# A decoder of four layers on one core: the order of the first loads, the clearing of the routing buffers, and the bias rows

## The chip, the cores and the metric

The kernel runs on one core of a Trainium2 chip. The metric is the device time of one execution in microseconds. A core has five engines that run side by side, each with its own stream of instructions in a fixed order: TensorE (PE, matrix products, with PEld for its weight loads), VectorE (DVE), ScalarE (ACT), GpSimd (POOL) and SyncE (SP), which here issues most of the transfers. An instruction that has to wait for a semaphore holds up everything behind it on its engine.

## The reference

The reference is a decoder on x of shape 8 x 256 x 256 (eight elements, 256 tokens, width 256) with a context of 8 x 256 x 192. It has four blocks, each of a self attention, a cross attention and a feed forward part; after each of these twelve parts the result is added to x and normalised:

```python
x = _layernorm(x + _L0_attn_ref(x, ...), axis=-1)
x = _layernorm(x + _L0_xattn_ref(x, ctx_768, ...), axis=-1)
x = _layernorm(x + _L0_ffn_ref(x, ...), axis=-1)
...
x = _layernorm(x + _L3_ffn_ref(x, ...), axis=-1)
return x
```

The kernel calls each of the twelve parts a layer and numbers them from 0 in the code. In the text of this document they are counted from one: layer one is `l0_attn` (16 heads of width 16, with biases on the queries, keys and values), layer two `l0_xattn` (one head, keys and values from the context), layer three `l0_ffn` (eight experts of width 512, all computed for all tokens and weighted by a softmax), layer four `l1_attn`, layer eight `l2_xattn`, layer ten `l3_attn` (its scores get a bias by relative position, looked up in a table of 32 buckets for 16 heads), layer eleven `l3_xattn` and layer twelve `l3_ffn` (two of eight experts for each token; the tokens are sorted by expert into a buffer in device memory, `slots`, and the results go to another, `given`).

## The kernel before

All eight elements of x stay on the core as tiles `xs[b]` (128 partitions, two halves of 128 tokens, 256 wide) through all layers. Besides them each layer keeps `xT`, the transposed x, in four tiles of two elements each. `transpose_x(b, name)` makes one element's share: four PE transposes of 128 x 128 into a bank of the accumulators (PSUM) and one copy out of it. Inside stretches whose DVE order is written out by hand (`order_of_text`) that copy is made by ACT; elsewhere `evac` alternates between DVE and ACT.

Weights come through a ring of six tiles of 1 MB each (`wtile`, `wload`, `wpart`, line 117 for all their transfers), so that SP runs ahead until a tile of the ring is still in use. Rows that are added along the tokens come through four smaller tiles (`load_row`, line 101), columns of biases through `load_cols` (line 95). All of these transfers, and those of x, the context and the clears, are issued by SP in one order; the program builder works it out before the run from the text and from when each transfer's target comes free, and it stands fixed in the program. The orders of PE, DVE, ACT and POOL are fixed in the same way, with those inside `order_of_text` taken from the text.

The start, before layer one: `hc`, a small table, and the eight x tiles are loaded (lines 90 and 108); then all eight elements are transposed (tiles `xtr_in`, `xT_in`), then the context, transposed (`ctxT`, lines 1754 and 1756, 2 MB; used by layers eight and eleven only). Layer one's weights follow (`w0a`, in the order wq, wk, wv, wo), then its bias columns and rows.

Layer one, `attention16` (called for layers one, four and seven), works on blocks of half an element: 16 blocks, each of four steps. `project_qk` and `proj_tok` make the queries, keys and values of the next element (tiles pk, pq, pv), `step` computes the scores twice, once with the queries along the partitions (s) for the row maxima (nm, by DVE) and once with the keys (t), on which ACT takes the exponential (eT); `turn_maxima` transposes the maxima on PE (ntr), `less_max` folds them into the queries (qm), `attend` multiplies the exponentials with the values and with ones (av), `normalise` divides. The previous element's output projection (po), addition of x (`add_x`; xb = x + bo by POOL), norm statistics (st, mv by DVE; ve and rs by POOL) and transposes (`finish`) are spread between the steps. The transposes of x, ntr and the projections take turns on one pair of PSUM banks in this layer.

The biases of the queries and keys are prepared by POOL (`kb`, lines 884 and 887). POOL also prepares columns for later layers when the builder places them early: `bqs` of layer two (line 914) and `bm` of layer four (line 870) stand, in POOL's order, ahead of the third element's xb and the first element's ve and rs.

Layer two begins, before its loop over elements, with `clear_slots` (lines 896 to 901): POOL sets a tile of the ring to zero, and SP writes it to the 16 MB of `slots` in 16 transfers of 1 MB and to the last 1 MB of `given` in a seventeenth. The products of layer twelve need this at the far end of the kernel.

Layer three goes over the eight experts, each with two tiles of the ring (w2a with Wg and Wu, w2b with Wd), and within an expert over four pairs of elements: pg and pu on PE, the product of the two on DVE, py on PE.

`relative_bias` runs at the start of layer eight: two small loads (`w9r`: a table of one-hot buckets and the embedding), one matmul (pb, line 1371), one copy, a transfer that writes the 16 resulting rows 128 times each to device memory (`lines`, 4 MB, line 1375), and four transfers that read windows of it, shifted by one from partition to partition, into the bias tile of layer ten (line 1379).

Of the kernel before, what the change touches and what calls it, by code (L numbers as in the profile page):

```python
# [11 lines left out]
F32 = mybir.dt.float32  # L12
# [7 lines left out]
P = 128  # L20
B, S, D, C = 8, 256, 256, 192
NT = S // P
# [10 lines left out]
def decoder_kernel(ctx: ExitStack, tc: tile.TileContext, t: dict, out: bass.AP, run=range(12)):  # L33
# [70 lines left out]

    xs = []
    for b in range(B):
        xb = xpool.tile([P, NT, D], F32, tag=f"x{b}", name=f"x{b}")
        nc.sync.dma_start(out=xb, in_=t["x"][b].rearrange("(t p) d -> p t d", p=P))
        xs.append(xb)
    xT = [None] * NB2  # L110
    xT_next = [None] * NB2

# [230 lines left out]
    ALL_KEYS = [(0, 0, S), (1, S, 2 * S)]  # L343


    def attention16(li, kind, wq, wk_, wv, wo, tabs=None, kbias=None, bv=None, bo=None, last=False):

# [9 lines left out]
        with tc.tile_pool(name=f"wk{li}", bufs=2) as wk:  # L357
# [164 lines left out]
            with order_of_text(mybir.EngineType.PE, mybir.EngineType.DVE):  # L522
                for k in (1, 0):
                    leave_qk(0, k, project_qk(0, k))
                for s in range(4):
                    step(-1, s)
                project_v(0)
                tr = turn_maxima(0)
                for e in range(2):
                    less_max(0, e, tr)  # L530
                for i, (b, c) in enumerate(blocks):
                    more = b + 1 < B
                    if c == 0:
                        step(i, 0, lambda: normalise(i - 1, 0))
                        normalise(i - 1, 1)
                        if more:
                            pk = project_qk(b + 1, 1)
                        step(i, 1)
                        if more:
                            leave_qk(b + 1, 1, pk)  # L540
                            pq = project_qk(b + 1, 0)
                    else:
                        step(i, 0)
                        if b > 0:
                            norm_scaled(ys.pop(b - 1))
                        attend(i - 1, 1, (1,))
                        step(i, 1, lambda: normalise(i - 1, 0))
                        normalise(i - 1, 1)
                        if more:
                            pv = proj_tok(wv, xTb(b + 1), 0, f"pv_{li}_{b + 1}")  # L550
                    step(i, 2)
                    if more:
                        if c == 0:
                            leave_qk(b + 1, 0, pq)
                        else:
                            leave_v(b + 1, pv)
                    if c == 1:
                        attend(i, 0, (0, 1))
                    elif b > 0:
                        po = project_out_mm([aTs.pop(b - 1)], wo, f"{li}_{b - 1}")  # L560
                        ys[b - 1] = add_x(wk, b - 1, po, bo, f"{li}_{b - 1}")
                    step(i, 3)
                    if c == 0:
                        attend(i, 0, (0, 1))
                    elif b > 0:
                        finish(b - 1, f"l{li}", last)
                    if i + 1 < len(blocks):
                        tr = turn_maxima(i + 1)
                        less_max(i + 1, 0, tr)
# [304 lines left out]
        return tabs  # L874

    def l0_attn(last):
        wq, wk_, wv, wo = weights16("w0a", [t[f"L0_attn_{n}"] for n in ("wq", "wk", "wv", "wo")])

        kbias = const.tile([P, 4, 2], F32, tag="kb0", name="kb0")
        for i, n in enumerate(("bq", "bk")):  # L880
            col = load_cols(f"L0_attn_{n}", 2)
            for e in range(2):
# [3 lines left out]
                if n == "bk":  # L886
                    nc.gpsimd.tensor_tensor(kbias[:, 2 + e, :], kbias[:, 2 + e, :],
                                            hc[:, 2 + e:3 + e].to_broadcast([P, 2]), ALU.add)
        attention16(0, "bias", wq, wk_, wv, wo, kbias=kbias.rearrange("p i c -> p (i c)"),
                    bv=load_row("L0_attn_bv", D), bo=load_row("L0_attn_bo", D), last=last)  # L890

    def clear_slots():

        routed["clear"] = True
        zero = wtile("zero")
        nc.gpsimd.memset(zero, 0.0)
        n = E8 * B * S // 16
        for i in range(16):
            nc.sync.dma_start(out=slots[i * n:(i + 1) * n].rearrange("(p r) d -> p (r d)", p=P), in_=zero)

        nc.sync.dma_start(out=given[ALWAYS * 256:].rearrange("(p r) d -> p (r d)", p=P), in_=zero)

    def l0_xattn(last):
        w = wtile("w0x")
# [8 lines left out]
        bqs = const.tile([P, 2], F32, tag="bqs1", name="bqs1")  # L913
        nc.gpsimd.tensor_scalar(bqs, bq, 1.0 / 16.0, None, ALU.mult)
        bv = load_row("L0_xattn_bv", D)
        clear_slots()
        with tc.tile_pool(name="wk1", bufs=3) as wk:
            for b in range(B):
                nm = f"1_{b}"
# [31 lines left out]
    def l0_ffn(last):  # L951
        NF = 4
        wr = load_router("L0_ffn_gate_w")
        with tc.tile_pool(name="wk2", bufs=2) as wk:
            gates = []
            for p in range(NB2):
# [401 lines left out]
            norm_and_transpose(b, xs[b], "l8", last)  # L1358
            xT[b // 2] = xT_next[b // 2]

    def relative_bias():

        W = S + P
        w = wtile("w9r")
        hot, emb, line = w[:32, 0:512], w[:32, 512:528], w[:16, 1024:1536]
        wload(hot, t["buckets"])
# [1 line left out]
        pb = bank("mm", "pb9")  # L1370
        nc.tensor.matmul(pb[:16, :], emb, hot, start=True, stop=True)
# [35 lines left out]
    def route_setup():  # L1407
# [20 lines left out]
        nc.gpsimd.iota(place_no, pattern=[[P, NT]], base=0, channel_multiplier=1,  # L1428
                       allow_small_or_imprecise_dtypes=True)
        if "clear" not in routed:  # L1430
            clear_slots()
# [308 lines left out]
    def ctx_weights(w, c0, n, wk_, wv):  # L1740
# [7 lines left out]
            got.append(w[tl][:, c:c + n])  # L1748
        return got

    with banks():
        for b in range(B):
            transpose_x(b, "in")
    nc.sync.dma_start(out=ctxT[:, 0, :], in_=t["ctxT"][0:P])
# [6 lines left out]
    pool9, rel9 = [], []  # L1761
    for i in run:
# [141 lines left out]
```

## Time and profile before

| what | value |
|---|---|
| median of three runs | 3599.01 us (3598.97 to 3599.45) |
| the profiled execution's own time | 3600.19 us |
| its span, first to last instruction | 3598.5 us |
| granted TensorE clock, mean | 0.972 |
| PE busy | 3361.3 us (93%) |
| DVE, ACT, POOL busy | 1643.1, 1054.2, 839.5 us |
| moved by the transfers | 168.37 MB |
| layer one's matmuls | from 21.50 us to 257 us |
| first matmul of layer three | 344.43 us |
| pb in layer eight | 2004.60 us |

The page of a profile gives busy times by engine and, in 40 slices of 90 us, how busy each engine and the transfers were. Of the other views, the timeline lists instructions in the order of time, with what ended the idle time before each; the waits add these idle times up; the windows give the busy times in chosen stretches. "SPq" is the issuing of a transfer by SP, which is not counted as busy; a transfer goes on long after its issue. An engine that waits costs nothing by itself. What costs is a wait that PE, which is the busiest engine throughout, takes over.

### The profile page before, as it was taken

To read this page: it belongs to the slowest core of one execution; us is meant where nothing else is said; L and a number is where in the kernel's file an instruction comes from. 1 tells how busy PE (TensorE), PEld (TensorE's weight loads), DVE (VectorE), ACT (ScalarE), POOL (GpSimd) and SP (SyncE) were. 2 spreads that over 40 slices of the span, in tenths; PEclk is the share of its full clock that TensorE was granted. 3 is DMA by queue.
4 is the path that set the end of the run, shared out by engine and by line. 5 is a ranking of instruction groups with operands and counts; after the bars stand their busy time and mean duration, and the time that the engine had idled before them with its cause. 6 is when DMAs were issued, how large, how long until landed. Compare 5 with 4: busy or idle time off the path is not lost. (4 is left out here: it accounts for less than half of the span.)

```text
span 3598.5 us, 49729 instructions
## 1 busy us (share of the span) xinstructions
PE 3361.3 (93%) x20476; PEld 2403.8 (67%) x20476; DVE 1643.1 (46%) x3154; ACT 1054.2 (29%) x2567; POOL 839.5 (23%) x883
## 2 busy tenths in 40 slices
PE   7989999999999978899998899899998999989998
PEld 4556655655556546688766676677776777768887
DVE  4764222222258756521388455766664454531003
ACT  3432111111113335532233342234343443321111
POOL 1000000000010046622122332222223343432214
PEclk8999899999999989999999999999999999999999
DMA  8000000000000001034300500100001000025542
GB/s 306 2 16 24 7 29 18 18 18 24 16 1 1 2 14 57 1 140 161 108 2 2 97 1 24 36 1 1 1 1 42 1 13 12 13 79 181 189 141 74
DMA packets 63386, 168.37 MB, mean 47 GB/s; under 512 B 7888, under 2 KB 38352, under 8 KB 51440
## 3 DMA queue, kind: packets, MB, share of 16 engines
q1 hardware_dynamic: 47408, 76.15, 7.1%
q0 software_dynamic: 15744, 88.94, 7.0%
q8 instruction: 166, 2.72, 0.3%
q14 instruction: 68, 0.56, 0.1%
HBM read 131.78 MB, written 33.29 MB: 46 GB/s over the span
## 5 line engine op out<-in xcount | busy, mean ns | idle before, releaser
L155 DVE TENSOR_REDUCE nm<-s 128x4 f32<-128x1024 f32 (+2 forms) x448 | 455.7, 1030 | 124.4 <-PE s L160 66.2
L610 POOL TENSOR_TENSOR ex<-ex,urc 128x1024 f32<-128x1024 f32 x192 | 363.3, 1893 | 622.9 <-DVE urc L155 610.9
L601 ACT ACTIVATE ex<-s,nm 128x256 f32<-128x256 f32 (+1 forms) x704 | 337.6, 492 | 341.7 <-DVE nm L155 319.0
L465 ACT ACTIVATE eT<-t 128x1024 f32<-128x1024 f32 (+1 forms) x192 | 182.6, 953 | 366.3 <-PE t L160 366.2
L851 PE MATMUL pu<-xT_l,w2a 128*128 128x512 f32 x512 | 244.4, 600 | 0.0
L851 PE MATMUL pg<-xT_l,w2a 128*128 128x512 f32 x512 | 242.0, 594 | 1.3 <-ACT sg L982 1.3
L160 PE MATMUL s<-qk,qk 32*128 32x256 f32 (+1 forms) x1536 | 218.9, 404 | 26.0 <-DVE nm L155 19.7
L983 DVE TENSOR_TENSOR h<-pu,sg 128x512 f32<-128x512 f32 x128 | 88.6, 692 | 337.2 <-PE pu L851 337.2
L982 ACT ACTIVATE sg<-pg 128x512 f32<-128x512 f32 x128 | 76.4, 597 | 565.7 <-PE pg L851 565.7
L836 PE MATMUL py<-w2b,h 128*128 128x256 f32 x1024 | 226.4, 379 | 0.0
L836 PEld LDWEIGHTS py<-w2b,h 128*128 128x128 f32 x1024 | 194.5, 190 | 40.4 <-issue 15.3
L163 PE MATMUL etr<-ident,ex 128*128 128x128 f32 x1568 | 211.0, 277 | 7.9 <-POOL ex L610 3.4
L160 PE MATMUL t<-qm,qk 32*128 32x256 f32 (+1 forms) x1536 | 207.7, 392 | 7.0 <-DVE nm L155 6.2
L163 PEld LDWEIGHTS etr<-ident,ex 128*128 128x128 f32 x1568 | 177.1, 141 | 51.6 <-issue 33.0
L160 PE MATMUL av<-eT,vg 128*64 128x256 f32 x1536 | 205.7, 393 | 1.7 <-ACT eT L175 1.1
L160 PE MATMUL s<-kg,qg 64*128 64x256 f32 x1280 | 177.9, 396 | 22.9 <-ACT qg L669 11.6
L160 PEld LDWEIGHTS s<-qk,qk 32*128 32x128 f32 x1536 | 126.6, 192 | 95.6 <-issue 49.3
L851 PEld LDWEIGHTS pu<-xT_l,w2a 128*128 128x128 f32 x512 | 98.1, 192 | 122.1 <-issue 122.1
L851 PEld LDWEIGHTS pg<-xT_l,w2a 128*128 128x128 f32 x512 | 97.0, 191 | 108.4 <-issue 105.2
L155 DVE COPY eT<-etr 128x1024 f32<-128x1024 f32 (+1 forms) x116 | 138.8, 1197 | 64.4 <-PE etr L163 64.4
L160 PEld LDWEIGHTS s<-kg,qg 64*128 64x128 f32 x1280 | 116.0, 187 | 74.6 <-ACT qg L669 26.9
L155 POOL TENSOR_SCALAR ve_l<-mv_l 128x2 f32<-128x2 f32 x104 | 23.6, 227 | 568.3 <-DVE mv_l L155 567.6
(336 smaller groups left out, 5949.1 us busy)
## 6 DMA issues: line engine op xcount, KB each, us to landing
slots<-zero SPq DMA_DIRECT2D x16, 1024.0 KB
given<-yo SPq DMA_DIRECT2D x19, 256.0 KB
w2a<-in_L_ffn_Wg SPq DMA_DIRECT2D x8, 512.0 KB
w2a<-in_L_ffn_Wu SPq DMA_DIRECT2D x8, 512.0 KB
w2b<-in_L_ffn_Wd SPq DMA_DIRECT2D x8, 512.0 KB
lines<-w9r SPq DMA_DIRECT2D x1, 4096.0 KB
bias<-lines SPq DMA_DIRECT2D x4, 768.0 KB
x<-in_x SPq DMA_DIRECT2D x8, 256.0 KB
```

The costliest lines, as they stand in the source:

```text
L155: return lambda *args, **kw: in_order(getattr(getattr(nc, self.engine), op)(*args, **kw))
L160: in_order(nc.tensor.matmul(*args, **kw))
L163: in_order(nc.tensor.transpose(*args))
L465: nc.scalar.activation(eT[:, :, :n], tt[:, :, :n], AF.Exp)
L601: nc.scalar.activation(ex[:, g, :], flat[:, g, :], AF.Exp, bias=nm[:, g:g + 1], accum_out=sums[:, g:g + 1])
L610: nc.gpsimd.tensor_tensor(ex, ex, rc[:, :nseg].unsqueeze(2).to_broadcast([P, nseg, 1024 // nseg]), ALU.mult)
L836: nc.tensor.matmul(py[:, q * D:(q + 1) * D], h[:, f, i * P:(i + 1) * P], w2[:, f, :], start=(f == 0), stop=(f == nf - 1))
L851: nc.tensor.matmul(ph, w1[:, c, f * P:(f + 1) * P], xT[p][:, c, :], start=(c == 0), stop=(c == 1))
L982: nc.scalar.activation(sg, pg, AF.Silu)
L983: nc.vector.tensor_tensor(h[:, f, :], pu, sg, ALU.mult)
```

## The change

Five things are moved; nothing is computed differently.

- The first loads. Only x0 is loaded at first and transposed before layer one. Layer one then loads wk and wq, the columns bq and bk, wv with its row bv, x1, wo with its row bo, and then x2 to x7.
- The transposes. x1 is transposed before the blocks of layer one start. x2 to x7 are transposed inside it by the new parameter `arrive` of `attention16`: in the second block of element b, ahead of step 1, for element b + 2. Their copies fall to ACT there.
- `ctxT` is loaded by `load_ctx` ahead of layer three.
- The clears. `clear_slots` gets a tile of layer three's own pool in place of a tile of the ring and returns its 17 transfers as a list; layer three issues one of them ahead of each pair of elements, from expert 0 on, until the list is empty.
- The bias rows. `relative_bias` is cut in two. Its first part, `relative_lines` (loads, matmul, copy, the writing of lines), is called by layer two in the place where the clears were; layer eight keeps the four windowed loads.

```diff
     for b in range(B):
-        xb = xpool.tile([P, NT, D], F32, tag=f"x{b}", name=f"x{b}")
-        nc.sync.dma_start(out=xb, in_=t["x"][b].rearrange("(t p) d -> p t d", p=P))
-        xs.append(xb)
+        xs.append(xpool.tile([P, NT, D], F32, tag=f"x{b}", name=f"x{b}"))
+
+    def bring(b):
+        nc.sync.dma_start(out=xs[b], in_=t["x"][b].rearrange("(t p) d -> p t d", p=P))
+
+    bring(0)
...
                         attend(i - 1, 1, (1,))
+                        if arrive is not None and b + 2 < B:
+                            arrive(b + 2)
                         step(i, 1, lambda: normalise(i - 1, 0))
...
     def l0_attn(last):
-        wq, wk_, wv, wo = weights16("w0a", [t[f"L0_attn_{n}"] for n in ("wq", "wk", "wv", "wo")])
+        w = wtile("w0a")
+
+        def part(i, n):
+            return wpart(w, 512 * i, 2, 256, t[f"L0_attn_{n}"])
+
+
+        wk_, wq = part(0, "wk"), part(1, "wq")
...
+        wv, bv = part(2, "wv"), load_row("L0_attn_bv", D)
+        bring(1)
+        wo, bo = part(3, "wo"), load_row("L0_attn_bo", D)
+        for b in range(2, B):
+            bring(b)
+
+        def arrive(b):
+            transpose_x(b, "in")
+            xT[b // 2] = xT_next[b // 2]
+
+        arrive(1)
...
-    def clear_slots():
+                    bv=bv, bo=bo, last=last, arrive=arrive)
+
+    def clear_slots(zero):
+

         routed["clear"] = True
-        zero = wtile("zero")
         nc.gpsimd.memset(zero, 0.0)
         n = E8 * B * S // 16
-        for i in range(16):
-            nc.sync.dma_start(out=slots[i * n:(i + 1) * n].rearrange("(p r) d -> p (r d)", p=P), in_=zero)
-
-        nc.sync.dma_start(out=given[ALWAYS * 256:].rearrange("(p r) d -> p (r d)", p=P), in_=zero)
+        parts = [slots[i * n:(i + 1) * n] for i in range(16)] + [given[ALWAYS * 256:]]
+        return [lambda to=to: nc.sync.dma_start(out=to.rearrange("(p r) d -> p (r d)", p=P), in_=zero)
+                for to in parts]
...
         bv = load_row("L0_xattn_bv", D)
-        clear_slots()
+        relative_lines()
...
+            clear = clear_slots(wk.tile([P, 2048], F32, tag="zero", name="zero", bufs=1))
             for e in range(E8):
...
                 for p in range(NB2):
+                    if e < 6:
+                        work_off(clear, 1)
...
-    def relative_bias():
-
-
-
-        W = S + P
+    def relative_lines():
+
         w = wtile("w9r")
...
-        bias = pool9[0].tile([P, 16, W], F32, tag="bias", name="bias9")
         lines = dram.tile([16, P, 512], F32, tag="lines", name="lines9")
         nc.sync.dma_start(out=lines, in_=line.unsqueeze(1).to_broadcast([16, P, 512]))
+        rel9.append(lines)
+
+    def relative_bias():
+
+
+        W = S + P
+        if not rel9:
+            relative_lines()
+        lines = rel9.pop()
+        bias = pool9[0].tile([P, 16, W], F32, tag="bias", name="bias9")
...
     with banks():
-        for b in range(B):
-            transpose_x(b, "in")
-    nc.sync.dma_start(out=ctxT[:, 0, :], in_=t["ctxT"][0:P])
-    for i in range(2):
-        nc.sync.dma_start(out=ctxT[64 * i:64 * i + 64, 1, :], in_=t["ctxT"][P:C])
+        transpose_x(0, "in")
...
+        if i > 1 and early:
+
+            load_ctx()
+            early = False
```

More of the change, by code (lines that the diff above doesn't have):

```diff
@@ L343, in decoder_kernel, with attention16 @@
     ALL_KEYS = [(0, 0, S), (1, S, 2 * S)]
-    def attention16(li, kind, wq, wk_, wv, wo, tabs=None, kbias=None, bv=None, bo=None, last=False):
+    def attention16(li, kind, wq, wk_, wv, wo, tabs=None, kbias=None, bv=None, bo=None, last=False,
+                    arrive=None):
         H, d = 16, 16
@@ L888, in l0_attn @@
                                             hc[:, 2 + e:3 + e].to_broadcast([P, 2]), ALU.add)
+        wv, bv = part(2, "wv"), load_row("L0_attn_bv", D)
[7 more added lines that the diff above has]
+        arrive(1)
         attention16(0, "bias", wq, wk_, wv, wo, kbias=kbias.rearrange("p i c -> p (i c)"),
-                    bv=load_row("L0_attn_bv", D), bo=load_row("L0_attn_bo", D), last=last)
-    def clear_slots():
+                    bv=bv, bo=bo, last=last, arrive=arrive)
+    def clear_slots(zero):
         routed["clear"] = True
-        zero = wtile("zero")
         nc.gpsimd.memset(zero, 0.0)
         n = E8 * B * S // 16
-        for i in range(16):
-            nc.sync.dma_start(out=slots[i * n:(i + 1) * n].rearrange("(p r) d -> p (r d)", p=P), in_=zero)
-        nc.sync.dma_start(out=given[ALWAYS * 256:].rearrange("(p r) d -> p (r d)", p=P), in_=zero)
+        parts = [slots[i * n:(i + 1) * n] for i in range(16)] + [given[ALWAYS * 256:]]
+        return [lambda to=to: nc.sync.dma_start(out=to.rearrange("(p r) d -> p (r d)", p=P), in_=zero)
+                for to in parts]
     def l0_xattn(last):
@@ L1430, in route_setup @@
         if "clear" not in routed:
-            clear_slots()
+            work_off(clear_slots(wtile("zero")))
         routed["keep"] = keep
@@ L1749, in ctx_weights, with load_ctx @@
         return got
+    def load_ctx():
+        nc.sync.dma_start(out=ctxT[:, 0, :], in_=t["ctxT"][0:P])
+        for i in range(2):
+            nc.sync.dma_start(out=ctxT[64 * i:64 * i + 64, 1, :], in_=t["ctxT"][P:C])
     with banks():
-        for b in range(B):
-            transpose_x(b, "in")
-    nc.sync.dma_start(out=ctxT[:, 0, :], in_=t["ctxT"][0:P])
-    for i in range(2):
-        nc.sync.dma_start(out=ctxT[64 * i:64 * i + 64, 1, :], in_=t["ctxT"][P:C])
+        transpose_x(0, "in")
+        if run[0] != 0:
+            for b in range(1, B):
+                bring(b)
+                transpose_x(b, "in")
     layers = [l0_attn, l0_xattn, l0_ffn, l1_attn, l1_xattn, l1_ffn,
@@ L1761, in decoder_kernel @@
     pool9, rel9 = [], []
+    early = True
     for i in run:
         xT[:] = xT_next
+        if i > 1 and early:
+            load_ctx()
+            early = False
         if i == 10:
```

## The prediction

> **What bounds the kernel now.** I read the page first, then the timeline of the first 40 us, the table of busy times over chosen windows, PE's waits, and the timelines around the places that the change touches.
>
> ```profile
> span 3598.5 us, 49729 instructions
> ...
> PE 3361.3 (93%) x20476; PEld 2403.8 (67%) x20476; DVE 1643.1 (46%) x3154; ACT 1054.2 (29%) x2567; POOL 839.5 (23%) x883
> ...
> DMA  8000000000000001034300500100001000025542
> ```
>
> PE is busy for 93% of the span, so a gain can only be idle time of PE that goes away. The DMA row shows where to look: the transfers fill one slice, the first 90 us.
>
> The timeline of the start (start us, length us, engine, line, operation; in brackets the idle time before it and what ended it):
>
> ```profile
> 1.25 4.00 SPq L108 DMA_DIRECT2D x<-in_x  x8
> ...
> 5.30 0.84 SPq L1754 DMA_DIRECT2D ctxT<-in_ctxT  x1
> ...
> 8.60 0.37 SPq L117 DMA_DIRECT2D w0a<-in_L_attn_wk  x1
> ...
> 10.76 0.34 SPq L95 DMA_DIRECT2D c_L_attn_bq<-in_L_attn_bq  x1
> ...
> 21.50 3.78 PE L160 MATMUL pk<-xT_in,w0a 128*128 128x256 f32 x8 [7.92 <-DMA w0a<-in_L_attn_wk]
> ...
> 25.38 1.93 ACT L383 ACTIVATE qk<-pk,kb,hc 128x256 f32<-128x256 f32 x4 [12.78 <-POOL xb L332]
> ```
>
> The reader is to see that the first projection, pk, waits for wk until 21.50. Eight x tiles and all of ctxT (2.1 MB each) and wq stand before wk in the one queue.
>
> Then the windows between successive transposes of the maxima (ntr, one per half element). Columns: window, length, busy time and count of PE, PEld, DVE, ACT, POOL, then clock, DMA share, GB/s:
>
> ```profile
> 51.55:63.78 12.23, 10.60 (x143) 6.30 (x139) 8.88 (x14) 4.09 (x4) 0.00 (x0) 1.00 1.01 424
> 63.78:77.95 14.17, 14.17 (x154) 9.27 (x155) 8.78 (x11) 7.73 (x12) 0.00 (x0) 1.00 0.98 398
> 77.95:95.30 17.35, 12.81 (x146) 7.36 (x143) 10.53 (x20) 4.29 (x5) 3.12 (x8) 0.90 0.18 45
> ...
> 121.70:135.88 14.18, 14.18 (x155) 9.28 (x155) 8.78 (x11) 8.01 (x13) 1.27 (x1) 1.00 0.00 1
> 135.88:148.11 12.23, 11.19 (x147) 6.71 (x143) 10.44 (x20) 4.29 (x5) 0.93 (x2) 1.00 0.01 1
> ```
>
> Halves of 14.17 and 12.23 us alternate; the one at 77.95 takes 17.35, that is 17.35 - 12.23 = 5.12 us too much. Its timeline says why:
>
> ```profile
> 80.96 0.34 POOL L870 TENSOR_TENSOR bm_L_attn_bq<-c_L_attn_bq,hc 128x2 f32<-128x2 f32 x2 [46.99 <-DMA c_L_attn_bq<-in_L_attn_bq]
> ...
> 84.48 0.72 POOL L155 TENSOR_TENSOR rs_l<-ve_l,nhalf 128x2 f32<-128x2 f32 x1
> 85.23 0.73 DVE L155 TENSOR_SCALAR x<-y,mv_l,rs_l 128x256 f32<-128x256 f32 x2 [3.51 <-POOL rs_l L155]
> ...
> 88.35 0.80 PE L160 MATMUL s<-qk,qk 32*128 32x256 f32 x2 [3.50 <-DVE nm L155]
> ```
>
> POOL had reached an early operation of layer four (bm), whose bias column stands on SP's queue behind the 17 clears of 1 MB. It sat there for 46.99 us; the first norm's rs was queued behind it, DVE waited 3.51 us, and PE 3.50.
>
> **The change part by part.**
>
> *First transfers.* In the built program's SP order, x1 is the ninth transfer: hc, x0, wk, wq, bq, bk, wv, bv, x1. On PE the transposes of x0 and x1 both stand before pk, so pk waits for x1, not x0 alone. Bytes up to x1: five of 0.262 MB and bv's 0.131, 1.44 MB. In the trace, windows of 1 us moved 0.45 MB by 4.0, 0.71 by 5, 1.02 by 6, 1.37 by 7, 1.70 by 8: 1.44 MB at 7.2. The first x had moved by 3.5 and released PE at 4.13, so 0.65 later: x1 at 7.9, and 0.3 for the small bq and bk makes 8.2. Its issue is no later limit: eight issues at 0.5 us after 0.80 reach 4.6, and 2.88 us (x0, 1.25 to 4.13) make 7.5. Four cold transposes take 0.97 (half of the row of eight, 1.94), and pk starts at 9.1 in place of 21.50: **-12.4**. Bounds: -13.0 (x1 at 7.5) to -10.2 (x1 at 10.3, if all after 4.0 us moved at the 187 GB/s of the slowest stretch, about 12 to 13 us). I take 8.2 because these loads are of the kind of the first x loads. The rest of the front moves along: kbias needs bq and bk (about 6.3) and then four products, vp's memset, a select and two adds, in all some 2.3 us of POOL, done by 8.6 and before pk's end at 12.9; in the trace too qk started at pk's end (25.28). What is late next is x1 itself, for 3 us on an idle PE.
>
> *Transposes inside layer one.* Six elements' 24 transposes and six copies leave the front, where they lay beside the wait for wk, and come into the shorter halves of the layer, after the sums (av<-eT,ones) and before the scores. The copies go to ACT (0.58 each), which idles 1.38 us at that place. On PE the trace shows this:
>
> ```profile
> 139.71 0.48 PE L160 MATMUL s<-qk,qk 32*128 32x256 f32 x2 [0.32 <-DVE nm L155]
> ...
> 146.72 0.66 PE L163 MATMUL xtr_l<-ident,x 128*128 128x128 f32 x4
> ...
> 2004.60 1.88 PE L1371 MATMUL pb<-w9r 32*16 32x512 f32 x2
> ```
>
> Four transposes hold PE for about 4 x 0.13 = 0.52 us ((0.66 - 0.27)/3 apart, 0.27 being one); 0.32 of it was waiting for DVE: 0.2 net, six times, **+1.2**. Bounds 0 (all swallowed by the 0.73 us that ntr later waits for DVE) and 6 x 0.66 = 4.0 (nothing hidden). The bank that each takes from the shared pair was read long before (pq's, two uses back), so I add no wait for it; were it not free, the cost would be a copy more (0.58) each.
>
> *Clears in layer three.* 17 transfers of 1 MB leave the queue before the second bq. What stands ahead of that column then is 9.0 MB of loads; at 187 to 430 GB/s it lands between some 22 and 50 us, and POOL's norm needs it at 80.2 - 12.4 = 68. The stall goes: **-5.12**, bounds -3.5 (only the wait itself, the slow clock after it staying) and -5.12. In the new place POOL's memset (1.81) comes after layer two's last rs and nothing on POOL waits behind it. On SP, expert 1's weights are queued behind lines, the memset and four clears. Layer two's last norm ends at 354.16, now 338; memset to 340; 4.2 MB of clears and 1.6 MB of weights at the 398 GB/s of the stretch with the clears are 14.5 us: landed by 357 with latency. Expert 0's last use of its w2a ended at 446.6 and expert 1's first pg ran at 453, now 437: 80 us of cover. If that cover were gone, every microsecond would be paid by PE. Do full DMA queues slow engines? The half of 14.17 us has the same length and the same PE time at a DMA share of 0.98 as at 0.00 (14.18). So **0**; from below no gain is excluded only for waits, and PE had none on these transfers; from above I keep +2.
>
> *Bias rows in layer two.* The pb product (1.88 cold, about 1 warm: four 128x512 products run in 1.88 in the stage of the experts) leaves the front of layer eight and comes into the front of layer two, both times right after a wait of 3.63 us on the norm. Its DVE copy (0.68) is followed there by no work that waits. The 4 MB of lines (44 us on the queue) block SP from 246 to about 290; behind them stand only the clears, which wait for 340. The windowed bias loads, formerly at 2052, are first used at 2284. **0**, bounds -1.9 and +1.9.
>
> *ctxT later* and SP's other reordering: first used at 2007: 0.
>
> Sum: -12.4 + 1.2 - 5.1 = -16.3. The profiled execution took 3600.19 (1.7 around its span), so 3583.9 in its own terms; the median of the runs is 1.18 below it: 3599.0 - 16.3 = 3582.7, say **3583**.
>
> The clock: the records show 0.50 at 20 to 24 us, 1.00 at 28 to 32, 0.70 at 32 to 36, so pk to ntr (14.92 us) ran partly cold, and I carry it over unchanged, with 1.5 us either way. The Trainium skill, TensorE: Matmul & The Clock Gate, "What's actually happening", has a free-running window of about 3.4 us, an idle one giving half speed. By an estimate from it the front could be 1.7 us shorter or longer by where the window falls, 3581.0 to 3584.4; the windows above agree with a step after idleness, their phase is not shown.
>
> **The rivals.**
> - *x1 is late and the front colder:* for it, the rates dip to 187 GB/s; against, they did so only once ctxT was moving. -10.2 + 1.5 + 1.2 - 5.1 = -12.6, 3586.4.
> - *The transposes hurt:* each costs its 0.66 and a bank wait of a copy, 1.24 x 6 = 7.4: -10.1, 3588.9. Against: the bank's earlier reader.
> - *POOL stays blocked:* the second bq lands after 68 us, below 136 GB/s in the mean: -11.2, 3587.8. Against: the rates.
> - *Slower:* expert 1's weights come late because the clears share their queue. The loss starts when they land after 437 and beats the gain after 453: 5.8 MB in 113 us, 51 GB/s against 398. Even at the rate of lines (4.2 MB in 44 us) they would be there at 401. Landing at 463: -16.3 + 26 = +9.7, 3608.7.
>
> **How the numbers follow.** Forecast 0.70 (3579.5 to 3586, from the bounds of the terms), x1 late 0.07, transposes 0.07, POOL 0.04, a larger gain (pb and clock both favourable, to 3577) 0.05, no net change by something not seen 0.04, slower 0.03. About 0.2%, 7.2 us, is what a measurement can tell from no change. Faster 0.93, same 0.04, slower 0.03. The range 3577 to 3589 takes in all cases but the last two.
>
> **What would show it.** Right: pk at about 9 with x as its last releaser; no 47 us wait of POOL; all halves of the first layer near 14.2 and 12.4; 16 clears between 340 and 395 with expert matmuls unbroken; pb at the front of layer two. Wrong: pk after 12; shorter halves above 12.9; a PE wait on w2a or w2b.

## The result

The change is faster, by what was forecast: the median of six runs is 3583.99 us, against 3599.16 for six of the kernel before beside them, a ratio of 0.9958 (95% interval 0.9945 to 0.9971), that is 15.2 us less (10.4 to 19.8). Forecast were 3583.0 us, within 3577 to 3589. Two later comparisons on other chips gave 0.9954 (0.9941 to 0.9968) and 0.9954 (0.9940 to 0.9967). Single runs of one kernel lie 10 us and more apart on one chip, and whole chips 10 us apart (the kernel before: 3590.5 on one, 3600.7 on another), so small effects are read from the traces here, at marks inside layer one, and only large ones from the times.

The profiled execution took 3581.02 us. Its page:

```profile
span 3579.3 us, 49731 instructions
...
PE 3348.3 (94%) x20476; PEld 2396.8 (67%) x20476; DVE 1640.1 (46%) x3150; ACT 1056.2 (30%) x2571; POOL 839.8 (23%) x883
...
DMA  4024400000000001044200100100001000025532
```

The full first slice of the transfers (8) is now a half full one (4). The clears that left it, and the bias rows, which left the 23rd slice (5 before, 1 now), stand in slices three to five, at layer two's front and in layer three. PE's instructions are the same in number.

The timeline of its start (start us, length us, engine, line, operation; in brackets the idle time before it and what ended it):

```profile
4.20 0.47 SPq L101 DMA_DIRECT2D c_L_attn_bv<-in_L_attn_bv  x1
...
4.26 1.09 PE L166 MATMUL xtr_in<-ident,x 128*128 128x128 f32 x4 [4.26 <-DMA x<-in_x]
4.71 0.43 SPq L110 DMA_DIRECT2D x<-in_x  x1
...
10.26 1.12 PE L166 MATMUL xtr_in<-ident,x 128*128 128x128 f32 x4 [4.90 <-DMA x<-in_x]
...
11.16 3.23 PE L163 MATMUL pk<-xT_in,w0a 128*128 128x256 f32 x8
...
14.47 1.28 ACT L387 ACT_TABLE_LOAD   x1 [14.47 <-PE pk L163]
...
15.77 1.93 ACT L387 ACTIVATE qk<-pk,kb,hc 128x256 f32<-128x256 f32 x4
```

pk starts at 11.16 in place of 21.50, not at 9.1. PE waits 4.90 us for x1, which was issued at 4.71 behind the row bv. And there is a line that the forecast doesn't have: ACT's table load, 1.28 us, now sits between the end of pk and the first qk. In the kernel before it ran at 0.80 us, beside the first loads, because the first thing that ACT did there was a copy of the transposes; with one element alone at the start that copy is DVE's, and ACT's first operation is the activation that needs pk. ACT's timeline of the kernel before:

```profile
0.80 1.28 ACT L168 ACT_TABLE_LOAD   x1 [0.80 <-PEq L1893]
```

The windows between successive ntr, whose columns are those of the forecast:

```profile
27.46:40.95 13.49, 11.66 (x115) 7.43 (x114) 6.57 (x10) 7.73 (x12) 0.87 (x5) 1.00 0.75 169
40.95:53.38 12.43, 11.12 (x146) 6.72 (x143) 8.88 (x14) 4.68 (x5) 0.00 (x0) 1.00 0.00 1
53.38:67.55 14.17, 14.17 (x154) 9.28 (x154) 8.78 (x11) 7.73 (x12) 1.29 (x1) 1.00 0.01 2
67.55:79.99 12.44, 11.71 (x151) 7.14 (x147) 10.44 (x20) 4.88 (x6) 0.96 (x2) 1.00 0.01 2
```

The half of 17.35 us is gone: it is the one of 12.44. The shorter halves are 0.20 to 0.21 longer than the 12.23 of before, which is the price of four transposes in each. The first of these halves took 15.13 before:

```profile
36.42:51.55 15.13, 13.50 (x116) 8.09 (x114) 6.57 (x10) 7.73 (x12) 0.00 (x0) 0.87 1.01 426
```

PE has about the same number of products in both. What differs is the clock, 1.00 in the mean against 0.87: by windows of 1 us it fell to 0.50 from about 47.3 to 50.7 us in the kernel before, after an idle stretch of PE, and stayed at 1.00 behind the same idle stretch in the changed one.

Why the stall is gone, on POOL's timeline:

```profile
38.55 0.34 POOL L876 TENSOR_TENSOR bm_L_attn_bq<-c_L_attn_bq,hc 128x2 f32<-128x2 f32 x2 [12.18 <-DMA c_L_attn_bq<-in_L_attn_bq]
...
70.07 0.24 POOL L158 TENSOR_SCALAR ve_l<-mv_l 128x2 f32<-128x2 f32 x1 [3.22 <-DVE mv_l L158]
70.40 0.72 POOL L158 TENSOR_TENSOR rs_l<-ve_l,nhalf 128x2 f32<-128x2 f32 x1
```

The column of layer four lands 31 us before the first norm needs POOL, and rs follows ve at once. The clears, by SP's timeline, now stand in layer three:

```profile
246.73 0.66 SPq L1396 DMA_DIRECT2D lines<-w9r  x1
341.20 3.07 SPq L922 DMA_DIRECT2D slots<-zero  x4
344.32 1.26 SPq L120 DMA_DIRECT2D w2a<-in_L_ffn_Wg  x1
...
348.32 4.45 SPq L922 DMA_DIRECT2D slots<-zero  x4
```

From 330 to 450 us no wait of PE names w2a or w2b; its only waits there are 3.5 us for a norm of layer two and 1.1 for the gate's activation.

From the start to layer one's last elements the difference adds up like this, after less before: pk -10.34; pk to the first ntr +1.38 (16.30 against 14.92); the next half -1.64 (13.49 against 15.13); the second +0.20; the stall -4.91, that is -5.12 and the +0.21 of that half. That is -15.31 at the fifth ntr (79.99 against 95.30). Four more halves with transposes add 0.83: SP's issue of layer four's row bo, which waits for a row tile that layer one gives free, comes at 199.84 in place of 214.32, **-14.48**. This issue is called the mark below. It is, in the kernel before and in the changed one:

```profile
214.32 0.34 SPq L101 DMA_DIRECT2D c_L_attn_bo<-in_L_attn_bo  x1
199.84 0.34 SPq L101 DMA_DIRECT2D c_L_attn_bo<-in_L_attn_bo  x1
```

### The profile page after: what moved, and what is told of

Its sections match the earlier page's. It is cut to its first block, busy times and chain, and to the rows that moved or that the text cites. A ratio compares the mean times of both kernels' runs of the same rounds, so it can differ in the third digit from the quotient of the medians.

```text
span 3579.3 us, 49731 instructions
## 1 busy us (share of the span) xinstructions
PE 3348.3 (94%) x20476; PEld 2396.8 (67%) x20476; DVE 1640.1 (46%) x3150; ACT 1056.2 (30%) x2571; POOL 839.8 (23%) x883
```

## The experiments

All were timed in five rounds beside the kernel before, those of one group on the same chip. Medians in us; the mark is from each one's profiled execution.

| kernel | median | before, same chip | ratio (95%) | mark |
|---|---|---|---|---|
| before | | | | 214.32 |
| front alone | 3604.01 | 3600.90 | 1.0004 (0.9995 to 1.0013) | 215.76 |
| clears alone | 3597.49 | 3600.90 | 0.9992 (0.9983 to 1.0001) | 207.18 |
| columns ahead | 3598.03 | 3600.90 | 0.9988 (0.9979 to 0.9997) | 207.91 |
| bias rows alone | 3601.56 | 3600.90 | 0.9998 (0.9989 to 1.0007) | 214.47 |
| changed kernel, second chip | 3574.07 | 3590.53 | 0.9954 (0.9941 to 0.9968) | 200.34 |
| x1 behind the projections | 3572.65 | 3590.53 | 0.9955 (0.9942 to 0.9969) | 196.41 |
| table load early | 3573.81 | 3590.53 | 0.9955 (0.9942 to 0.9969) | 199.07 |
| x1 ahead of wv | 3564.77 | 3590.53 | 0.9933 (0.9919 to 0.9946) | 198.75 |
| changed kernel, third chip | 3584.03 | 3600.66 | 0.9954 (0.9940 to 0.9967) | 200.70 |
| both at the front | 3580.73 | 3600.66 | 0.9940 (0.9927 to 0.9954) | 194.48 |
| clears twice | 3582.78 | 3600.66 | 0.9948 (0.9934 to 0.9961) | 200.88 |
| front and columns ahead | 3589.15 | 3600.66 | 0.9968 (0.9956 to 0.9980) | 199.29 |

### The front alone

```diff
-        relative_lines()
+        work_off(clear_slots(wtile("zero")))
         with tc.tile_pool(name="wk1", bufs=3) as wk:
...
-            clear = clear_slots(wk.tile([P, 2048], F32, tag="zero", name="zero", bufs=1))
             for e in range(E8):
...
-                    if e < 6:
-                        work_off(clear, 1)
```

> The new order of the first loads, the transposes inside layer one and the later load of the context, with the clears left in layer two and the bias rows in layer eight. Theory: the third element's norm needs POOL at about 69 us now, but the bias column of layer four still stands behind the clears with nearly the same bytes ahead of it and lands at 80 to 84 us (80.96 in the kernel before); so the 12 to 14 us won at the front are given back in one longer stall, and the time is that of the kernel before within about 3 us: 3596 to 3602. Rival, gains that add up (-10.3 for the first projection, +1.4, -1.6 and +1.3 behind it, the stall of 5 staying as long as it was): -9 to -10, 3589 to 3590.

Measured: no change in time, and the mark 1.44 us later than in the kernel before. POOL's timeline of this run:

```profile
70.51 0.23 POOL L158 TENSOR_SCALAR ve_l<-mv_l 128x2 f32<-128x2 f32 x1 [3.23 <-DVE mv_l L158]
83.90 0.35 POOL L876 TENSOR_TENSOR bm_L_attn_bq<-c_L_attn_bq,hc 128x2 f32<-128x2 f32 x2 [13.17 <-DMA c_L_attn_bq<-in_L_attn_bq]
84.20 0.71 POOL L158 TENSOR_TENSOR rs_l<-ve_l,nhalf 128x2 f32<-128x2 f32 x1
```

and its waits of PE in layer one (total, times, longest):

```profile
PE s L163 <- DVE nm L158: 18.9, 6, 13.0
```

The norm comes 10 us earlier, and POOL stands before the same column, which lands at 83.90 in place of 80.96. The stall of 3.50 us on PE has become one of 13.0, and the half around it takes 27.93 us in place of 17.35:

```profile
67.99:95.92 27.93, 14.21 (x151) 8.09 (x147) 10.55 (x20) 4.88 (x6) 1.81 (x7) 0.76 0.51 124
```

What is won at the front is only passed on to the next thing that is late. So the rival that adds up the parts falls: the front is worth nothing while the column stands behind the clears.

### The clears alone

The same edit of `clear_slots` and layer three as in the change, on the kernel before:

```diff
         bv = load_row("L0_xattn_bv", D)
-        clear_slots()
...
+            clear = clear_slots(wk.tile([P, 2048], F32, tag="zero", name="zero", bufs=1))
             for e in range(E8):
...
+                    if e < 6:
+                        work_off(clear, 1)
```

> The kernel before with only the clears moved into layer three. Theory: the wait of POOL for the bias column ends long before the first norm, the half of 17.35 us becomes one of 12.2, and nothing else moves: -5.1 us, 3594 (3592 to 3596). Rival, the clears cost in layer three what they spare in layer one (weights late, slower engines beside a full queue): 3597 or more. Rival, the stall has another releaser than the column: no change, 3599.

### Three columns ahead of the clears

```diff
         bv = load_row("L0_xattn_bv", D)
+        ahead_cols.update({n: load_cols(n, k) for n, k in (("L1_attn_bq", 2), ("L1_attn_bk", 2), ("L1_xattn_gains", 10))})
         clear_slots()
```

> The kernel before with one thing changed: the three small loads of columns of layer four (queries, keys, gains) are issued ahead of the clears, which stay in layer two. Theory, the stall is POOL waiting for a column that is queued on SP behind the clears: it goes as fully as where the clears themselves go, -5.1 us, 3594 (3592 to 3596). Rival, the stall comes from the 17 MB of traffic itself, which slows the engines: no change, 3599.

Measured, both together, since they end the same stall by different means: in both the long half is gone. Windows of the run with the columns ahead, the clears being where they were (same columns as above):

```profile
62.48:76.65 14.17, 14.17 (x154) 9.27 (x155) 8.78 (x11) 7.73 (x12) 1.28 (x1) 1.00 1.00 391
76.65:88.88 12.23, 11.19 (x146) 6.72 (x142) 10.44 (x20) 4.29 (x5) 0.96 (x2) 1.00 0.31 85
```

With the clears moved the same two halves took 14.17 and 12.24. So the half of 17.35 loses 5.12 and 5.11 us, and the traffic of the clears, which fills the first of the two windows (share 1.00, 391 GB/s), slows nothing: it is the place of a column of some bytes in a queue that cost 5.1 us. At the mark the two are 7.14 and 6.41 earlier; beyond the stall, 1.3 of the 6.41 and 2.0 of the 7.14 come from the start (first and second ntr at 35.10 and 50.14, and at 36.05 and 49.50, against 36.42 and 51.55). With the columns ahead wk came 1.52 earlier (pk at 19.98); with the clears moved the half after the first ntr had the better clock (13.45 in place of 15.13).

In the whole time the medians fall by 3.4 and 2.9 us only, by their ratios 2.9 (-0.4 to 6.1) and 4.3 (1.1 to 7.6). The forecast of 5.1 lies in both intervals, the mark's 7.1 does not lie in the first. Where after layer one some microseconds were lost is not settled.

### The bias rows alone

```diff
         clear_slots()
+        relative_lines()
         with tc.tile_pool(name="wk1", bufs=3) as wk:
```

> The kernel before with only the first part of the bias rows (two loads, the matmul pb, its copy, the writing of the lines) moved from layer eight to layer two. Theory: 0, with pb 0.9 us shorter on a warm clock and 1.9 us gone from one front and put into another: 3599 (3597 to 3601). Rival, the remaining front of layer eight was bounded by the lines and their windows, and layer eight gets shorter by more than 2 us: 3596 or less. Rival, the lines block the weights of layer three on SP's queue: 3602 or more.

Measured: +0.7 in the medians, -0.7 by the ratio, with an interval of 3.2 us either way: no change that can be told. pb took 1044 ns a matmul at layer two's front, as it did in layer eight before, and 592 in the changed kernel. Neither rival shows.

This run shows something else about the kernel before, whose layer one it shares. Its start happened to be quicker: the fourth ntr stood at 74.75 in place of 77.95. But the fifth came at 95.44 in place of 95.30, because POOL waited for the column until 81.47:

```profile
74.75:95.44 20.69, 13.37 (x146) 7.58 (x143) 10.54 (x20) 4.29 (x5) 3.05 (x8) 0.84 0.20 61
```

So in the kernel before it is the column, and not the start, that sets the fifth ntr, and the stall's 5.12 us are the size that it had in one execution.

### x1 behind the first projections

```diff
-        arrive(1)
         attention16(0, "bias", ...)
...
                 project_v(0)
+                if arrive is not None:
+                    arrive(1)
                 tr = turn_maxima(0)
```

> The changed kernel with the four transposes of x1 moved behind the first element's projections, so that pk waits for x0, wk and kb alone. Theory: the 4.90 us that PE waited for x1 ahead of pk go, pk starts at 6.2 instead of 11.16, and the first ntr comes 4 to 5 us earlier: 4 to 5 us below the changed kernel. Rival, the next thing is late at once (kb of POOL at 8.4, wv and its row, the table load of ACT): the first ntr comes at most 2 us earlier.

Timeline of PE in this run:

```profile
6.11 3.78 PE L163 MATMUL pk<-xT_in,w0a 128*128 128x256 f32 x8 [0.79 <-DVE xT_in L158]
...
22.77 1.06 PE L166 MATMUL xtr_in<-ident,x 128*128 128x128 f32 x4
24.55 0.41 PE L166 MATMUL ntr<-ident,nm 128*128 128x128 f32 x2 [0.72 <-issue]
```

pk starts 5.18 us earlier than in the changed kernel on the same chip (11.29), the first ntr 3.42 (24.55 against 27.97) and the mark 3.93. Of the 5.18, 1.78 are lost again behind pv, where the transposes of x1 now stand: 1.06 for them and a gap of 0.72 before ntr. The table load (9.96) is still on the path. In the whole time only 1.4 us are seen, which the spread doesn't tell from 4 or from 0.

### The table load early

```diff
+        elif (name, b) == ("in", 0):
+            nc.scalar.copy(dst, src)
         else:
             leave(dst, src)
```

> The changed kernel with the copy of x0's transposes made by ACT in place of DVE. Theory: ACT's table load of 1.28 us, which in the changed kernel waits until pk has ended (14.47) since the first activation stands there, comes at the start of the kernel again, and the first qk follows pk at once: qk at 14.5 in place of 15.77, the first ntr 1.3 us earlier, 1.3 us below the changed kernel. Rival, the load stays beside other work of PE (pq runs until 16): no change.

ACT's timeline:

```profile
0.80 1.28 ACT L212 ACT_TABLE_LOAD   x1 [0.80 <-PEq L1936]
...
15.00 1.93 ACT L389 ACTIVATE qk<-pk,kb,hc 128x256 f32<-128x256 f32 x4 [8.73 <-DMA x<-in_x]
```

In this run x1 came 0.50 later (pk at 11.79 against 11.29), but pk ended at the same time (14.90 against 14.91), and qk starts 1.28 us earlier than beside it (15.00 against 16.28), the first ntr 1.28 earlier (26.69 against 27.97), and the mark 1.27. The load's whole 1.28 us were on the path. The rival (cover by pq) falls; the time itself (-0.3 in the medians) can't show it.

### x1 ahead of wv

```diff
-        wv, bv = part(2, "wv"), load_row("L0_attn_bv", D)
         bring(1)
+        wv, bv = part(2, "wv"), load_row("L0_attn_bv", D)
```

> The changed kernel with x1 loaded ahead of wv and the row bv. Theory, the slow stretch of the transfers (100 to 120 GB/s, 6 to 8.7 us) belongs to the row bv, which is spread over all partitions, and it delays x1: x1 lands 1.5 to 2.5 us earlier (pk at 8.7 to 9.7 in place of 11.16), and the slow stretch comes after it; 1.5 to 2.5 us below the changed kernel. Rival, the slow stretch belongs to the small columns bq and bk or to the early time itself: x1 gains only the 0.39 MB that it is moved ahead of at 300 GB/s and more, pk 1.0 to 1.3 us earlier, and the slow stretch stays at 6 to 8 us.

x1's transposes start at 7.30 and pk at 8.21, 3.08 us earlier than beside it, more than expected. Windows of 1 us of this run, the last three columns being clock, share of the transfer engines and GB/s:

```profile
6.00:7.00 1.00, 0.00 (x0) 0.00 (x0) 0.23 (x1) 0.00 (x0) 0.92 (x5) 1.00 0.91 314
7.00:8.00 1.00, 0.69 (x3) 0.70 (x4) 0.00 (x0) 0.00 (x0) 1.00 (x4) 1.00 0.58 176
8.00:9.00 1.00, 1.00 (x4) 0.89 (x4) 0.54 (x1) 0.00 (x0) 1.00 (x4) 1.00 0.46 128
9.00:10.00 1.00, 1.00 (x4) 0.75 (x3) 0.15 (x1) 0.00 (x0) 0.67 (x3) 1.00 0.51 163
10.00:11.00 1.00, 1.00 (x4) 0.82 (x3) 0.00 (x0) 0.00 (x0) 0.00 (x0) 1.00 1.11 327
```

and of the first profile of the changed kernel:

```profile
6.00:7.00 1.00, 0.00 (x0) 0.00 (x0) 0.08 (x1) 0.00 (x0) 0.69 (x5) 1.00 0.81 183
7.00:8.00 1.00, 0.00 (x0) 0.00 (x0) 0.00 (x0) 0.00 (x0) 1.00 (x2) 1.00 0.68 104
8.00:9.00 1.00, 0.00 (x0) 0.00 (x0) 0.00 (x0) 0.00 (x0) 1.00 (x5) 1.00 0.80 198
9.00:10.00 1.00, 0.00 (x0) 0.00 (x0) 0.00 (x0) 0.00 (x0) 0.89 (x3) 1.00 1.04 363
```

The slow stretch lay ahead of x1 and now lies behind it, where wv, bv, wo and bo follow: it belongs to those loads and not to the hour, and not to the columns bq and bk, which are where they were and leave a shorter dip, 100 to 190 GB/s from 5.0 to 5.8. Matrices of the same shape as wv and wo (wq, wk) went ahead of it at 275 and 339 GB/s (the windows from 4 to 5 us of the two runs), which leaves the rows, spread from one row of 1 KB over 128 partitions. A row that has the queue to itself shows the same. Layer four's row bo is such a one: in the changed kernel it is issued at 199.84, with a transfer share of 0.00 before and after it. The first window below is its whole transfer; the second is the first stretch of layer four's weights, matrices of 256 KB that find the queue as empty:

```profile
200.75:202.75 2.00, 2.00 (x34) 1.18 (x33) 1.65 (x5) 0.00 (x0) 0.00 (x0) 1.00 0.27 74
844.75:845.50 0.75, 0.75 (x5) 0.65 (x4) 0.00 (x0) 0.00 (x0) 0.00 (x0) 1.00 0.56 195
```

Either moves some 0.15 MB, the row in 2 us and the matrices in 0.75. So the row by itself is slow, and with no other load beside it. Why it is, no run shows.

Of the 3.08 us at pk, 1.59 are left at the mark: the half after the first ntr took 15.04 here and 13.49 in the changed kernel. The whole time, on the other hand, is 9.3 us lower in the medians, with all five runs at or below the lowest of the five beside it. 7.7 of that is not made in layer one. In the profiled runs, which are 10.5 apart, 4.5 lie between the mark and the load of layer four's table (650.74 against 655.25), stages in which nothing differs between the two kernels, and in which two other profiles of the changed kernel took 650.82 and 650.95. So part of this gain may be no property of the order; that is open.

### The changed kernel again, both edits at the front, the clears twice, and the front with the columns ahead

> The changed kernel once more, beside the three variants of it that follow, so that they are compared on one chip. Theory: 15 us below the kernel before, as in its first runs (3584.0 against 3599.2), with pk at 11.2 us, ntr of the first half at 27.5, and no wait of PE above 6 us in layer one.

> The changed kernel once more, so that the three runs after it stand beside it on their own chip. Theory: 15 to 16 us below the kernel before, as twice so far (15.2 and 16.5).

Both about as expected in time (-16.5, -16.6) and in the trace (pk at 11.29 and 11.84, first ntr at 27.97 and 28.32).

Both edits of the front together, the diffs of "x1 behind the first projections" and "the table load early":

```diff
-        arrive(1)
         attention16(0, "bias", ...)
...
                 project_v(0)
+                if arrive is not None:
+                    arrive(1)
...
+        elif (name, b) == ("in", 0):
+            nc.scalar.copy(dst, src)
```

> The changed kernel with x1's transposes behind the first projections and x0's copy made by ACT, that is both of the single edits that moved the first ntr (-3.93 and -1.27 us). Theory, the two waits lie on one chain and add up: pk at 6.2, qk at 9.5, first ntr 5.2 us earlier than in the changed kernel, about 22.8 us, and 5 us below it in time, as far as the clock at the starts of later stages lets that be seen. Rival, without the table load the qk activations wait for kb (POOL, 8.4 to 8.7) or PE's later matmuls for wv and its row: the first ntr comes 4 us earlier at most.

PE's timeline:

```profile
6.02 3.78 PE L163 MATMUL pk<-xT_in,w0a 128*128 128x256 f32 x8 [0.68 <-ACT xT_in L212]
9.60 2.80 PE L163 MATMUL pq<-xT_in,w0a 128*128 128x256 f32 x8
13.05 1.16 PE L163 MATMUL s<-qk,qk 32*128 32x256 f32 x16 [0.66 <-ACT qk L389]
```

pk at 6.02, qk at 9.90, first ntr at 22.62, 5.70 earlier than in the changed kernel beside it, and the mark 6.22 earlier: the two waits were on one chain and add up (3.42 and 1.28 at the first ntr by themselves; the changed kernel beside this run also had x1 0.55 later than the one beside those two). The time is 19.9 us below the kernel before in the medians, by the ratio 21.6 (16.6 to 26.3), and 3.3 below the changed kernel; the intervals of those two overlap. It beats the kernel before clearly, and the changed kernel by its marks; in time the two can't be told apart.

The clears twice:

```diff
-                for to in parts]
+                for to in parts + parts]
...
                     if e < 6:
-                        work_off(clear, 1)
+                        work_off(clear, 2)
```

> The changed kernel with each of the 17 clears of layer three issued twice, 34 MB in place of 17. Theory, the clears are fully hidden there: expert 1's weights stand behind 8 MB of clears, 9.6 MB at 398 GB/s are 24 us, landed by about 370 us where the matmuls need them at 437, so no wait of PE on w2a or w2b, and the time is the changed kernel's within 2 us. Rival, the slower end of the prediction: full queues slow the engines or the weights come late, then twice the clears cost at least as much again as the first did, more than 2 us, and a wait of PE on w2a or w2b shows.

SP's timeline, and behind it the waits of PE from 330 to 460 us:

```profile
344.59 8.27 SPq L922 DMA_DIRECT2D slots<-zero  x8
352.91 1.25 SPq L120 DMA_DIRECT2D w2a<-in_L_ffn_Wg  x1
...
356.96 15.09 SPq L922 DMA_DIRECT2D slots<-zero  x8
```

```profile
PE xtr_l L166 <- DVE x L158: 4.1, 2, 3.5
PE pg L857 <- ACT sg L1007: 1.2, 1, 1.2
```

Expert 1's weights are issued behind eight clears, and no matmul waits for them. The median is 1.3 us below that of the changed kernel beside it. The profiled execution was the slowest of its five (3592.20; the others 3580.72 to 3583.39), but the stretch that holds layer three, from the mark to the load of layer four's table, took 653.84 there, within the 650.82 to 655.25 of the changed kernel's three profiles. Seventeen megabytes more cost nothing that can be measured: the clears are hidden in layer three with room to spare.

The last run is the front alone (its diff stands above), with the columns loaded ahead of the clears:

```diff
-        relative_lines()
+        ahead_cols.update({n: load_cols(n, k) for n, k in (("L1_attn_bq", 2), ("L1_attn_bk", 2), ("L1_xattn_gains", 10))})
+        work_off(clear_slots(wtile("zero")))
```

> The front of the changed kernel with the clears left in layer two and the bias rows in layer eight, as in the run of the front alone, but with the three small loads of layer four's columns issued ahead of the clears. Theory, the gain of the front was lost only because POOL's queue waited for these columns: the wait of 13 us of PE goes, layer one ends 14 to 16 us earlier than in the kernel before, and the time is that of the changed kernel (15 us below the kernel before) though the clears haven't moved. Rival, the 17 MB of clears beside layer one's first elements hold the front back as well (x2 to x7, layer two's weights): less than 10 us below the kernel before.

The wait of 13.0 us is gone (PE's longest for nm in layer one is 1.5), the column is there at 26.86, and the mark is at 199.29, 15.03 below the kernel before: in layer one, loading three columns first gives all that moving 17 MB of clears gives. In the whole time the median is 11.5 us below the kernel before (7.2 to 15.8), 5.1 above the changed kernel beside it. Its profiled execution, 3584.05, is within 1 us of that kernel's, 3584.67. The interval reaches the expected 15, but all three kernels that keep the bias rows in layer eight and end the stall show 2 to 4 us less in the whole time than at the mark. Moving the rows alone gained nothing, and the two profiles don't point at them: this run leads the changed kernel by 2.32 us at the load of layer four's table (849.33 against 851.65) and has lost that by the load of layer seven's wq (1718.42 against 1717.97), where nothing differs between the two; the stretch with layer eight's front takes 451.51 and 451.23 (to layer ten's Wk). Where the microseconds go is left open.

## Why the prediction was right, and where its steps were off

The time was forecast within 1 us, and the signs and causes held; but two terms of the front were off, and the agreement to a microsecond is partly luck. The sum's 16.3 us all lay ahead of the mark, where the three profiles of the changed kernel show 14.48, 13.98 and 13.62; the medians are 15.2, 16.5 and 16.6 lower. The 0.7 to 3 us between the two arise behind the mark, where the sum had nothing, and no run says from what.

- **First transfers, -12.4; measured -10.34 at pk and -8.96 at the first ntr.** The step that failed is the landing of x1. It was priced by bytes, at the rate of the first x loads, with 0.3 us for the small ones; the row bv was counted as 0.131 MB. In the run the stretch with the row moved 104 to 198 GB/s with the transfer engines at 0.68 to 0.81, and x1 landed at 10.26 in place of 8.2. The lower bound of the term (x1 at 10.3) is what came; the choice of the middle was wrong, because the loads in front of x1 were not "of the kind of the first x loads". The run with x1 ahead of wv shows it: 3.08 us at pk, of which wv's own 0.262 MB, at some 300 GB/s, would be 0.9 by an estimate. The kernel before showed it too: its slowest stretch was not the one at 187 GB/s but that of the rows bv and bo (by the bytes moved until then, 5.3 MB, it is their turn), with the transfer engines at 0.39 and 0.65:

```profile
21.00:22.00 1.00, 0.50 (x1) 0.50 (x2) 0.00 (x0) 0.00 (x0) 0.00 (x0) 0.50 0.39 116
22.00:23.00 1.00, 1.00 (x4) 0.73 (x4) 0.00 (x0) 0.00 (x0) 0.00 (x0) 0.50 0.65 115
```

- **The rest of the front "moves along"**: it didn't quite. Who makes the first element's copy changes when the transposes are cut from eight elements to one, and with it where ACT's table load stands. That is 1.28 us on the path, shown by the run that puts it back; no term of the sum had it. The page ScalarE: Activation LUTs of the Trainium skill, "What ACT_TABLE_LOAD costs", gives 1283 ns for the load, and the trace's 1.28 agrees; it adds a drain of about 1380 ns for every switch to a different set, of which no row here shows anything, since qk starts 0.02 us after the load's end.
- **Transposes inside layer one, +1.2; measured +1.24** (0.20, 0.21 and four more that add 0.83): the working by 0.52 of PE less a wait of 0.32 was right, and no bank was waited for.
- **The stall, -5.12; measured -5.12 and -5.11** in the two single edits, and -4.91 with that half's transposes in the changed kernel. The cause is shown twice over: three columns moved alone end it, and the front moved alone makes PE's wait 13.0 us.
- **Clears in layer three, 0; measured 0** to within the spread even when they are doubled, so the rival that ends slower falls with the weights' wait that it needs.
- **Bias rows and the later context, 0; measured 0.7 us, either sign, of 3.2.** pb in the changed kernel is on a warm clock (1.03 for the two in place of 1.88).
- **The clock, 1.5 either way; measured 1.6 in one place.** The half after the first ntr takes 13.45 to 13.50 us in some executions and 15.04 or 15.13 in others, whether its start is the old or the new one, by whether the granted clock falls to 0.50 for some 3.4 us in its later part. All three profiles of the changed kernel had the short half, which made up for the table load in the difference. The kernel before had the long one, which cost it nothing in the end: with the short one, in the run of the bias rows, the column still set the fifth ntr. The forecast's estimate of 1.7 us, from the Trainium skill, TensorE: Matmul & The Clock Gate, "What's actually happening", agrees with that step of 1.6.

The terms stand in a sum, but they are not each worth what they say when made alone: the front alone gave 0, the clears alone about 3, the front with the columns ahead 11.5, and all five parts together 15 to 17. The forecast came out right because it asked whether the column would land by the norm's new time, 68 us, and not only by the old one.

## What to carry to other kernels

When the start of a kernel is made shorter, ask which queue will be late next: here a column of a few bytes, needed only three layers on, stood behind 17 MB in one queue and ahead of a norm in another, and would have taken back the whole gain. Price small loads and rows spread over partitions by the time that the trace shows for their kind, not by bytes, and put them behind the transfer that the first matmul needs. When an engine loses its first operation, see what came with that operation: its table load moves to the next one that it does.

## What the runs showed of the hardware that was not expected

- A load of one row of 1 KB spread over 128 partitions (0.131 MB) took 2 us with the queue to itself, at 74 GB/s in the mean and a transfer share of 0.27. Among matrices of 256 KB, the stretch with two such rows ran at 128 to 176 GB/s and a share of 0.46 to 0.58, against 314 to 327 GB/s around it, and the transfer that was queued behind wv and a row came 3 us earlier when it was put ahead of them.
- The first table load can stand behind a wait: where ACT's first operation was the activation of qk, the load came at 14.47 us, after pk, though ACT had been idle since the start. Where it was a copy, the load came at 0.80 us, though the copy itself waited until 8.40 (kernel before) or 5.69 (the run with the table load early). What makes the difference between the two is not shown.
- The same instructions took 650.82 to 655.25 us between the mark and the load of layer four's table in three profiled executions of the changed kernel. A gain of 4 us at the front could be seen in a trace's marks (3.93 with x1 behind the projections), and not in five runs' times (1.4).
